# A two-layer graph network: PSUM banks and order of work where one layer hands over to the next

## The chip, the cores and the metric

The kernel runs on one NeuronCore of a Trainium2 chip. The metric is the time of one execution on the device, in microseconds; lower is better. The kernel before takes 3890.02 us (median of three runs, 3889.3 to 3892.25).

## The reference

Eight graphs of 2048 nodes with 256 features share one adjacency matrix. Layer 0 is attention with four heads of 64, in which the softmax is taken separately within each of eight chunks of 256 keys and the chunks' results are added; then come an output projection, a residual and two layer norms. Layer 1 is graph attention with additive scores, a residual and a norm.

```python
# layer 0
q, k, v = x @ Wq.T + bq, x @ Wk.T + bk, x @ Wv.T + bv        # per head
scores = clip(einsum('bhnd,bhjcd->bhnjc', q, kc) / 8, -10, 10)
scores = where(mask == 0, -10, scores)
ctx = einsum('bhnjc,bhjcd->bhnd', softmax(scores, -1), vc)    # softmax per chunk
out = layernorm(ctx @ Wo.T + bo + x) * gamma + beta
x = layernorm(x + out)
# layer 1
Wh = x @ W                                                     # per head
e = leaky_relu(s_src[:, :, None, :] + s_dst[:, None, :, :])    # masked with adj
x = layernorm(x + elu(einsum('bijh,bjhd->bihd', softmax(e, 2), Wh)))
```

## The kernel before

The work goes batch by batch (`b`, eight of them). A batch has 64 slots of layer 0: four blocks of 512 queries, two pairs of heads, eight chunks of keys. In a slot TensorE makes the next slot's scores (L360), VectorE clips and masks them (L371), ScalarE takes the exponential (L383), and TensorE multiplies by the values (`product`, L393), once per head of the pair. `normalize` (L408 to L417) divides by the sums on VectorE and GpSimd. Beside this, each slot carries three tiles of layer 1 of the batch before: VectorE makes `e` (L689), TensorE multiplies (`use`, L709). Layer 1 goes in twelve units; the end of a unit (`close`) has four steps: `dn` on VectorE (L732, L733), `hh` on ScalarE (L737, the last reader of the unit's PSUM bank `pa`), `ee` and `hp` on ScalarE (L741, L743), and `h` on VectorE (L745). `lower.rest(n)` takes n of these steps.

Between the last slot of a batch and the first of the next lies the **change of layers**, written out by hand as a list of steps (`order`). In it the next batch's four blocks are projected (load `l`, turn `t` on VectorE at L274, keys `k` and queries `q` at L304, values `v` at L320, with ScalarE drains at L312 and L327), while the last block of queries of the batch at hand is finished: its context is turned on TensorE and copied by ScalarE (`ctx`, L441 and L444), projected (`po`, L508), added to its input (L519), normed twice (statistics on VectorE at L458 to L467, GpSimd at L468 and L469, apply on ScalarE at L473), turned (`pt`, L283, copied at L286) and multiplied by layer 1's weights (`pw`, L552, drained at L559 and L563). Then `factors` makes layer 1's score factors. The seventh batch is followed by the eighth; after the eighth, layer 1 runs alone, with another list of steps.

Each engine runs its instructions in the order in which the program emits them. [...]`psA` has two tiles of two banks each (scores, the projections, `po`, `pt`, `pw`), `psC` one bank (`product`), `psL` two tiles of one bank (layer 1's `pa`, and at the program's start the masks' `pm`), `psM` one bank. A new tile of a pool waits until the readers of the earlier tile in its place are done.

At the start of the program the first batch's blocks are projected with a step of `Masks` between every two pieces: six or five transposes of the adjacency on TensorE (`pm`, L229), `clip` on VectorE (L231), `edge` on ScalarE (L233), and the next `ab` on VectorE (L219).

Of the kernel before, what the change touches and what calls it, by code (L numbers as in the profile page):

```python
# [8 lines left out]
F32 = mybir.dt.float32  # L9
# [4 lines left out]
AF = mybir.ActivationFunctionType  # L14
# [3 lines left out]
P = 128  # L18
CH = 512
# [3 lines left out]
def adj_resnorm_kernel(  # L23
# [19 lines left out]
    nc = tc.nc  # L43
    B, N, F = x.shape
    H, D = a_src.shape
    NT = N // P
    NCH = N // CH
    KC = F // P
# [7 lines left out]
    QT = CH // P  # L56
# [7 lines left out]
    SLOTS = NCH * QS  # L64
# [17 lines left out]
    psA = ctx.enter_context(tc.tile_pool(name="psA", bufs=2, space=bass.MemoryType.PSUM))  # L82
    psC = ctx.enter_context(tc.tile_pool(name="psC", bufs=1, space=bass.MemoryType.PSUM))
    psL = ctx.enter_context(tc.tile_pool(name="psL", bufs=2, space=bass.MemoryType.PSUM))
# [16 lines left out]
    qT = big.tile([P, KC, N], F32, tag="qT", name="qT")  # L101
    kT = big.tile([P, KC, N], F32, tag="kT", name="kT")
# [30 lines left out]
    wk_sb = weights(wkT, "wk_sb")  # L133
# [155 lines left out]
    def project(b, g):  # L289

        cols = slice(g * CH, (g + 1) * CH)
        st = {}

        def load():
            st["x"] = load_turned(x, b, g, "xp")

        def turn():
            st["xT"] = turned(st["x"], "xT")

        def linear(dst, w, bias):  # L300
            pp = psA.tile([P, KC, CH], F32, tag="psA", name="pp")
            for c in range(KC):
                for kc in range(KC):
                    nc.tensor.matmul(  # L304
                        pp[:, c, :],
                        lhsT=w[:, kc, c * P : (c + 1) * P],
                        rhs=st["xT"][:, kc, :],
                        start=(kc == 0),
                        stop=(kc == KC - 1),
                    )  # L310
            for c in range(KC):
                nc.scalar.activation(  # L312
                    dst[:, c, cols], pp[:, c, :], AF.Identity, bias=bias[:, c : c + 1]
                )

        def values():
            pv = psA.tile([P, QT, F], F32, tag="psA", name="pv")
            for u in range(QT):
                for kc in range(KC):
                    nc.tensor.matmul(  # L320
                        pv[:, u, :],
                        lhsT=st["xT"][:, kc, u * P : (u + 1) * P],
                        rhs=wv_sb[:, kc, :],
                        start=(kc == 0),
                        stop=(kc == KC - 1),
                    )
            nc.scalar.copy(  # L327
                vaug[:, QT * g : QT * (g + 1), :, :D],
                pv.rearrange("p t (h d) -> p t h d", h=H),
            )  # L330

        return [
            load,
            turn,
            lambda: linear(kT, wk_sb, bk_sb),
            values,
            lambda: linear(qT, wq_sb, bq_sb),
        ]


    where = [(s // QS, s % QS // NK, s % NK) for s in range(SLOTS)]
# [60 lines left out]
    def normalize(s):  # L402

        q, hp, c = where[s]
        raw = raws.pop(s)
        del probs[s]
        rd = small.tile([P, 2, QT, 1], F32, tag="rd", name="rd")
        nc.vector.reciprocal(rd, raw[:, :, :, D:D1])  # L408
        if c == 0:
            accs[q, hp] = small.tile([P, QT, 2, D], F32, tag="acc", name="acc")  # L410
        accv = accs[q, hp].rearrange("p t k d -> p k t d")
        part = accv
        if c:
            part = small.tile([P, 2, QT, D], F32, tag="part", name="part", bufs=1)
        nc.gpsimd.tensor_mul(part, raw[:, :, :, :D], rd.to_broadcast([P, 2, QT, D]))  # L415
        if c:
            nc.gpsimd.tensor_add(accv, accv, part)  # L417
# [435 lines left out]
    lower = None  # L853
    for b in range(B):
        waug = blocks.tile([P, NT, H, D1], F32, tag="waug", name="waug")
        sd = small.tile([P, 2 * H, NT], F32, tag="sd", name="sd", bufs=1)
        if b == 0:
            for s in range(3):
                load_slab(s)
        scores(0)  # L860
        for u in range(KT):
            exps(0, u)
        if lower:
            for _ in range(STEP):
                lower.make()
        closing = Closing(b - 2, CLOSING) if b > 1 else None
        if closing:
            closing.do(-1)
        group = None
        for s in range(SLOTS):  # L870
            q, hp, c = where[s]
            i = s % QS
            send()
            if s + 3 < SLOTS:
                load_slab(s + 3)
            if i == 0:
                before = group
                group = Between(b, q - 1, sd, waug) if q else None
            if i == 1 and q:
                load_context(b, q - 1, 1)  # L880
            if i == QS // 2 + 1:
                load_context(b, q, 0)
            if group and i in AHEAD:
                AHEAD[i](group)
            if s == SLOTS - 1 and b + 1 < B:
                turns = [project(b + 1, g) for g in range(NCH)]
                turns[0].pop(0)()
            if s:
                normalize(s - 1)
            if s + 1 < SLOTS:  # L890
                scores(s + 1)

            if i == 3 and q:
                turn_context(q - 1, 1)
            if i == QS // 2 + 3:
                turn_context(q, 0)
            if group:
                for step in BESIDE.get(i, ()):
                    step(group)
            elif closing:  # L900
                closing.do(s, behind=False)
            product(s, 0)
            if s + 1 < SLOTS:
                for u in range(KT):
                    exps(s + 1, u)
            if lower:
                if b + 1 < B or s < SLOTS - LATE:
                    lower.step()
            elif masks.left():
                masks.step()  # L910
            product(s, 1)

            if before and i in AFTER:
                AFTER[i](before)
            if i == 0 and q:
                send_context(b, q - 1, 1)
            if i == QS // 2:
                send_context(b, q, 0)
            if group and i in BEHIND:
                BEHIND[i](group)  # L920
            elif closing and not q:
                closing.do(s, beside=False)
        normalize(SLOTS - 1)
        if lower and b + 1 < B:
            lower.rest(4)

        send()
        before = group
        gd, fs = factors(b, sd, waug)
        group = None  # L930
        every = tuple(range(QT))

        def begin():
            nonlocal group
            group = Between(b, NCH - 1, sd, waug)

        def ctx():
            context(NCH - 1, 1)

        steps = [  # L940
            lambda: group.bias(),
            lambda: group.output(every),
            lambda: group.add(every),
            lambda: (group.shift(), group.a.stats(every)),
            lambda: group.a.apply(group.y),
            lambda: (group.scale(), group.again(), group.b2.stats(every)),
            lambda: group.finish(),
            lambda: group.turn_all(),
            lambda: group.values((0, 1)),
            lambda: group.values((2, 3)),  # L950
        ]
        if b + 1 < B:
            (t0, k0, v0, q0), (l1, t1, k1, v1, q1), (l2, t2, k2, v2, q2), (l3, t3, k3, v3, q3) = turns
            order = [begin, t0, lambda: before.values((2, 3)), steps[0], k0, ctx, l1, v0, steps[1]]
            order += [t1, steps[2], q0, *steps[3:5], k1, l2, steps[5], v1, steps[6], t2, q1, l3]
            order += [steps[7], k2, steps[8], steps[9], v2, fs[0], t3, q2, fs[1], k3]
            order += [lambda: [load_slab(s) for s in range(3)], fs[2], v3, q3]
        else:

            step = lower.step  # L960
            order = [begin, lambda: before.values((2, 3)), steps[0], step, ctx, step, steps[1], step]
            order += [steps[2], step, steps[3], step, steps[4], step, steps[5], step, steps[6], step]
            order += [steps[7], step, steps[8], step, steps[9], step, fs[0], step, fs[1], step, fs[2]]
            order += [step, lambda: lower.rest(4)]
            assert sum(p is step for p in order) == LATE
        for piece in order:
            send()
            piece()
        send()
        lower = Layer1(b, gd, waug)  # L970
# [56 lines left out]
```

## Time and profile before

| what | value |
|---|---|
| time, median of three | 3890.02 us |
| span of the profiled run | 3888.7 us |
| TensorE busy | 3696.5 us |
| VectorE busy | 3204.7 us |
| ScalarE busy | 1946.2 us |
| last change of layers, first `pw` to first product of the next batch | 3178.00 to 3241.86 us |
| keys/queries drain, 128x512 (L312) | 0.683 us each |
| values drain, 128x1024 (L327) | 1.013 us |
| turn of a block on VectorE, 128x1024 (L274) | 1.243 us |

A timeline line gives start and duration in us, engine, line, operation, output and inputs with their shape, and how many instructions are merged; in brackets the time that the engine was idle ahead of it and what ended the wait. TensorE's ends are modelled, so the distance from start to start tells more than a duration does. Names: `pp` is a projection of keys (`wk_sb`) or queries (`wq_sb`), `pv` of values.

### The profile page before, as it was taken

To read this page: it belongs to the slowest core of one execution; us is meant where nothing else is said; L and a number is where in the kernel's file an instruction comes from. 1 tells how busy PE (TensorE), PEld (TensorE's weight loads), DVE (VectorE), ACT (ScalarE), POOL (GpSimd) and SP (SyncE) were. 2 spreads that over 40 slices of the span, in tenths; PEclk is the share of its full clock that TensorE was granted. 3 is DMA by queue.
4 is the path that set the end of the run, shared out by engine and by line. 5 is a ranking of instruction groups with operands and counts; after the bars stand their busy time and mean duration, and the time that the engine had idled before them with its cause. 6 is when DMAs were issued, how large, how long until landed. Compare 5 with 4: busy or idle time off the path is not lost. (4 is left out here: it accounts for less than half of the span.)

```text
span 3888.7 us, 160154 instructions
## 1 busy us (share of the span) xinstructions
PE 3696.5 (95%) x72068; PEld 2752.5 (71%) x72068; DVE 3204.7 (82%) x4810; ACT 1946.2 (50%) x3601; POOL 1384.4 (36%) x1202
## 2 busy tenths in 40 slices
PE   7988999999999999999999999999999999999787
PEld 4655577776777767776777767777677776776676
DVE  4776499985999779996999959998599977998798
ACT  3655445554555445554555545555455555555321
POOL 0444234342433333432433324434243333434310
PEclk9999999999999999999999999999999999999999
DMA  7642333333434343333433334333343334333354
GB/s 151 150 108 59 77 96 98 97 89 94 121 97 102 75 121 101 99 102 70 134 99 100 97 87 129 101 95 88 94 121 102 98 78 118 106 95 88 95 146 123
DMA packets 771328, 398.48 MB, mean 102 GB/s; under 512 B 442576, under 2 KB 735824, under 8 KB 770640
## 3 DMA queue, kind: packets, MB, share of 16 engines
q1 hardware_dynamic: 720640, 354.54, 35.9%
q10 hardware_dynamic: 50000, 33.70, 2.7%
q8 instruction: 563, 9.22, 1.0%
q14 instruction: 125, 1.02, 0.1%
HBM read 331.22 MB, written 56.89 MB: 100 GB/s over the span
## 5 line engine op out<-in xcount | busy, mean ns | idle before, releaser
L371 DVE SCALAR_TENSOR_TENSOR pr<-ps,slab 128x1024 f32<-128x1024 f32 x1024 | 1192.7, 1205 | 237.3 <-PE ps L360 234.0
L393 PEld LDWEIGHTS pc<-vaug,pr 128*64 128x64 f32 x32768 | 1041.6, 138 | 475.3 <-ACT raw L400 243.9
L689 DVE SCALAR_TENSOR_TENSOR e<-srow,gd,et 128x640 f32<-128x640 f32 (+1 forms) x1536 | 1348.0, 934 | 5.4 <-PE pa L709 5.4
L393 PE MATMUL pc<-vaug,pr 128*64 128x65 f32 x32768 | 1161.4, 224 | 68.9 <-ACT raw L400 63.1
L383 ACT ACTIVATE pr<-pr 128x1024 f32<-128x1024 f32 x1024 | 1052.1, 1057 | 249.3 <-DVE pr L371 234.5
L709 PE MATMUL pa<-waug,e 128*64 128x65 f32 x32768 | 1089.8, 224 | 41.0 <-DVE e L689 39.2
L709 PEld LDWEIGHTS pa<-waug,e 128*64 128x64 f32 x32768 | 1025.2, 139 | 70.3 <-DVE e L689 39.8
L360 PE MATMUL ps<-qT,kT 64*128 64x512 f32 x4096 | 1022.4, 617 | 9.1 <-DVE pr L371 7.0
L415 POOL TENSOR_TENSOR part<-raw,rd 128x512 f32<-128x512 f32 x448 | 467.9, 1044 | 1472.7 <-DVE rd L408 1460.1
L400 ACT COPY raw<-pc 128x260 f32<-128x260 f32 x1024 | 383.5, 375 | 1139.0 <-PE pc L393 1092.4
L417 POOL TENSOR_TENSOR acc<-acc,part 128x512 f32<-128x512 f32 x448 | 574.0, 1281 | 35.2
L360 PEld LDWEIGHTS ps<-qT,kT 64*128 64x128 f32 x4096 | 351.5, 186 | 332.1 <-issue 208.7
L408 DVE RECIPROCAL rd<-raw 128x8 f32<-128x8 f32 x512 | 101.5, 198 | 139.4 <-ACT raw L400 133.2
L415 POOL TENSOR_TENSOR acc<-raw,rd 128x512 f32<-128x512 f32 x64 | 66.8, 1043 | 366.1 <-DVE rd L408 365.3
L304 PE MATMUL pp<-xT,wk_sb 128*128 128x512 f32 x256 | 123.9, 628 | 47.0 <-DVE xT L274 32.3
L737 ACT ACTIVATE hh<-pa,dn 128x64 f32<-128x64 f32 x512 | 114.0, 319 | 101.3 <-DVE dn L733 101.3
L552 PE MATMUL pw<-w_sb,x1T 128*128 128x264 f32 x512 | 137.0, 403 | 2.6 <-DVE x1T L274 2.5
L468 POOL TENSOR_TENSOR rs_c<-rs_c,nhalf 128x4 f32<-128x4 f32 x32 | 55.6, 1738 | 227.5 <-DVE off_c L467 227.5
L508 PE MATMUL po<-wo_sb,qT 128*128 128x256 f32 x512 | 124.8, 389 | 0.0
L304 PEld LDWEIGHTS pp<-xT,wk_sb 128*128 128x128 f32 x256 | 48.3, 198 | 106.5 <-issue 49.6
L320 PE MATMUL pv<-wv_sb,xT 128*128 128x256 f32 x512 | 115.9, 379 | 0.0
L304 PE MATMUL pp<-xT,wq_sb 128*128 128x512 f32 x256 | 115.3, 593 | 0.0
(90 smaller groups left out, 1888.2 us busy)
## 6 DMA issues: line engine op xcount, KB each, us to landing
et<-edgeD SPq DMA_DIRECT2D x256, 320.0 KB, 3.2
slab<-clipD SPq DMA_DIRECT2D x512, 128.0 KB, 3.5
et<-edgeD SPq DMA_DIRECT2D x128, 384.0 KB, 3.5
srow<-rowD SPq DMA_DIRECT2D x64, 320.0 KB, 4.4
xp<-in_x_dram SPq DMA_DIRECT2D x256, 64.0 KB, 2.3
xg<-in_x_dram SPq DMA_DIRECT2D x32, 512.0 KB, 4.7
x1D<-y ACTq DMA_DIRECT2D x32, 512.0 KB, 3.1
x1g<-x1D SPq DMA_DIRECT2D x32, 512.0 KB, 5.9
```

Of the source, the lines that this page charges most:

```text
L304: nc.tensor.matmul(pp[:, c, :], lhsT=w[:, kc, c * P : (c + 1) * P], rhs=st["xT"][:, kc, :], start=(kc == 0), stop=(kc == KC - 1),)
L360: nc.tensor.matmul(ps[:, k, :], lhsT=kT[rows, hp, t * P : (t + 1) * P], rhs=qT[rows, hp, cols], start=True, stop=True,)
L371: nc.vector.scalar_tensor_tensor(pr, pss[u], -CLIP, slab[:, u, :].unsqueeze(1).to_broadcast([P, 2, CH]), op0=ALU.max, op1=ALU.min,)
L383: nc.scalar.activation(pr, pr, AF.Exp, scale=0.125)
L393: nc.tensor.matmul(pc[z * D : (z + 1) * D, i, :], lhsT=probs[s][u][:, k, i * P + z * D : i * P + (z + 1) * D], rhs=vaug[:, KT * c + u, 2 * ...
L400: nc.scalar.copy(raws[s][:, k], pc)
L415: nc.gpsimd.tensor_mul(part, raw[:, :, :, :D], rd.to_broadcast([P, 2, QT, D]))
L417: nc.gpsimd.tensor_add(accv, accv, part)
L508: nc.tensor.matmul(po[:, k, :], lhsT=qT[:, c, t * P : (t + 1) * P], rhs=wo_sb[:, c, :], start=(c == 0), stop=(c == KC - 1),)
L552: nc.tensor.matmul(pw[:, k, : F + 2 * H], lhsT=self.x1T[:, c, u * P : (u + 1) * P], rhs=w1_sb[:, c, :], start=(c == 0), stop=(c == KC - 1),)
L689: nc.vector.scalar_tensor_tensor(e[:, :w], self.rows[n][:, :w], self.gd[:, h, j : j + 1], self.edge[k // JG][:, j % JG, :w], op0=ALU.max, ...
L709: nc.tensor.matmul(self.pa[z * D : (z + 1) * D, i * D1 : (i + 1) * D1], lhsT=e[:, i * P + z * D : i * P + (z + 1) * D], rhs=self.waug[:, j ...
```

## The change

Four things are done together, all at the change of layers. Values and queries leave `psA` and go through layer 1's two one-bank tiles (`psL`), half a block at a time, each half drained as soon as its matmuls are done; keys stay in `psA`, also drained half by half. The first block of the next batch is loaded at slot 61 rather than 63 and turned in slot 63, ahead of the change. The end of layer 1's last unit, which was taken in one go ahead of the change, is spread over it. And `normalize` of the last slot moves behind the first keys. The aim is that TensorE should not wait for the first turn nor for the drains of the two-bank tiles. The same `project` also serves the first batch at the program's start, where `psL` carries the masks.

```diff
-        def linear(dst, w, bias):
+        def linear(dst, w, bias, c, pp):
+            for kc in range(KC):
+                nc.tensor.matmul(pp, lhsT=w[:, kc, c * P : (c + 1) * P], rhs=st["xT"][:, kc, :], ...)
+            nc.scalar.activation(dst[:, c, cols], pp, AF.Identity, bias=bias[:, c : c + 1])
+
+        def keys():
             pp = psA.tile([P, KC, CH], F32, tag="psA", name="pp")
             for c in range(KC):
-                for kc in range(KC):
-                    nc.tensor.matmul(pp[:, c, :], ...)
-            for c in range(KC):
-                nc.scalar.activation(dst[:, c, cols], pp[:, c, :], ...)
+                linear(kT, wk_sb, bk_sb, c, pp[:, c, :])
+
+        def queries():
+            for c in range(KC):
+                linear(qT, wq_sb, bq_sb, c, psL.tile([P, CH], F32, tag="psL", name="pq"))
 
         def values():
-            pv = psA.tile([P, QT, F], F32, tag="psA", name="pv")
-            for u in range(QT):
-                ...
-            nc.scalar.copy(vaug[:, QT * g : QT * (g + 1), :, :D], ...)
+            for u0 in range(0, QT, 2):
+                pv = psL.tile([P, 2, F], F32, tag="psL", name="pv")
+                for u in range(2):
+                    ...
+                t = QT * g + u0
+                nc.scalar.copy(vaug[:, t : t + 2, :, :D], ...)
...
-            if s == SLOTS - 1 and b + 1 < B:
+            if s == SLOTS - 3 and b + 1 < B:
                 turns = [project(b + 1, g) for g in range(NCH)]
                 turns[0].pop(0)()
             if s:
                 normalize(s - 1)
+            if s == SLOTS - 1 and b + 1 < B:
+                turns[0].pop(0)()
             if s + 1 < SLOTS:
                 scores(s + 1)
...
-        normalize(SLOTS - 1)
-        if lower and b + 1 < B:
-            lower.rest(4)
...
-            order = [begin, t0, lambda: before.values((2, 3)), steps[0], k0, ctx, l1, v0, steps[1]]
+            rest = [lambda: lower.rest(1)] if lower else []
+            norm = lambda: normalize(SLOTS - 1)
+            order = [begin, *rest, k0, norm, lambda: before.values((2, 3)), *rest, l1, v0, *rest, ctx]
+            order += [steps[0], steps[1], *rest]
             order += [t1, steps[2], q0, *steps[3:5], k1, l2, steps[5], v1, steps[6], t2, q1, l3]
             order += [steps[7], k2, steps[8], steps[9], v2, fs[0], t3, q2, fs[1], k3]
```

In the list, `steps[0]` adds the output bias to the input, `steps[1]` is the output product `po`, `steps[2]` the add, `steps[3:5]` the first norm, `steps[5]` scale, second residual and its statistics, `steps[6]` the second norm's apply and the store, `steps[7]` the turn `pt`, `steps[8]` and `steps[9]` the two halves of `pw`, and `fs` the factors.

More of the change, by code (lines that the diff above doesn't have):

```diff
@@ L298, in turn @@
             st["xT"] = turned(st["x"], "xT")
-        def linear(dst, w, bias):
+        def linear(dst, w, bias, c, pp):
+            for kc in range(KC):
+                nc.tensor.matmul(
+                    pp,
+                    lhsT=w[:, kc, c * P : (c + 1) * P],
+                    rhs=st["xT"][:, kc, :],
+                    start=(kc == 0),
+                    stop=(kc == KC - 1),
+                )
+            nc.scalar.activation(dst[:, c, cols], pp, AF.Identity, bias=bias[:, c : c + 1])
@@ L301, in linear @@
+        def keys():
             pp = psA.tile([P, KC, CH], F32, tag="psA", name="pp")
             for c in range(KC):
-                for kc in range(KC):
[L304 to L310, printed above, removed]
-            for c in range(KC):
-                nc.scalar.activation(
-                    dst[:, c, cols], pp[:, c, :], AF.Identity, bias=bias[:, c : c + 1]
-                )
@@ L316, in values @@
-        def values():
-            pv = psA.tile([P, QT, F], F32, tag="psA", name="pv")
-            for u in range(QT):
[L319 to L338, printed above, removed]
+                linear(kT, wk_sb, bk_sb, c, pp[:, c, :])
+        def queries():
+            for c in range(KC):
+                linear(qT, wq_sb, bq_sb, c, psL.tile([P, CH], F32, tag="psL", name="pq"))
+        def values():
+            for u0 in range(0, QT, 2):
+                pv = psL.tile([P, 2, F], F32, tag="psL", name="pv")
+                for u in range(2):
+                    for kc in range(KC):
+                        nc.tensor.matmul(
+                            pv[:, u, :],
+                            lhsT=st["xT"][:, kc, (u0 + u) * P : (u0 + u + 1) * P],
+                            rhs=wv_sb[:, kc, :],
+                            start=(kc == 0),
+                            stop=(kc == KC - 1),
+                        )
+                t = QT * g + u0
+                nc.scalar.copy(
+                    vaug[:, t : t + 2, :, :D], pv.rearrange("p t (h d) -> p t h d", h=H)
+                )
@@ L341, in adj_resnorm_kernel @@
+        return [load, turn, keys, values, queries]
     where = [(s // QS, s % QS // NK, s % NK) for s in range(SLOTS)]
@@ L952, in adj_resnorm_kernel @@
         if b + 1 < B:
-            (t0, k0, v0, q0), (l1, t1, k1, v1, q1), (l2, t2, k2, v2, q2), (l3, t3, k3, v3, q3) = turns
-            order = [begin, t0, lambda: before.values((2, 3)), steps[0], k0, ctx, l1, v0, steps[1]]
+            (k0, v0, q0), (l1, t1, k1, v1, q1), (l2, t2, k2, v2, q2), (l3, t3, k3, v3, q3) = turns
+            rest = [lambda: lower.rest(1)] if lower else []
+            norm = lambda: normalize(SLOTS - 1)
+            order = [begin, *rest, k0, norm, lambda: before.values((2, 3)), *rest, l1, v0, *rest, ctx]
+            order += [steps[0], steps[1], *rest]
             order += [t1, steps[2], q0, *steps[3:5], k1, l2, steps[5], v1, steps[6], t2, q1, l3]
@@ L960, in adj_resnorm_kernel @@
             step = lower.step
+            normalize(SLOTS - 1)
             order = [begin, lambda: before.values((2, 3)), steps[0], step, ctx, step, steps[1], step]
```

## The prediction

> **What bounds the kernel now.** I read the page's first part, then the timeline of TensorE around the seven changes of layers, then VectorE's and ScalarE's there, and last the start of the program.
>
> ```profile
> PE 3696.5 (95%) x72068; PEld 2752.5 (71%) x72068; DVE 3204.7 (82%) x4810; ACT 1946.2 (50%) x3601; POOL 1384.4 (36%) x1202
> ```
>
> TensorE is busy 95% of the span; only its idle time can be won. One change of layers (the last) on TensorE, number in brackets the idle time ahead and its releaser:
>
> ```profile
> 3178.00 2.94 PE L552 MATMUL pw<-w_sb,x1T 128*128 128x264 f32 x12
> 3183.26 3.70 PE L304 MATMUL pp<-xT,wk_sb 128*128 128x512 f32 x8 [2.32 <-DVE xT L274]
> ...
> 3190.69 3.62 PE L508 MATMUL po<-wo_sb,qT 128*128 128x256 f32 x16
> 3194.14 3.60 PE L304 MATMUL pp<-xT,wq_sb 128*128 128x512 f32 x8
> 3199.10 3.70 PE L304 MATMUL pp<-xT,wk_sb 128*128 128x512 f32 x8 [1.35 <-ACT qT L312]
> ...
> 3211.79 3.70 PE L304 MATMUL pp<-xT,wk_sb 128*128 128x512 f32 x8 [0.94 <-ACT qT L312]
> ...
> 3238.34 2.16 PE L360 MATMUL ps<-qT,kT 64*128 64x512 f32 x8 [0.30 <-ACT qT L312]
> 3240.80 1.13 PE L360 MATMUL ps<-qT,kT 64*128 64x512 f32 x4 [0.30 <-DVE pr L371]
> ```
>
> Five gaps, 2.32 + 1.35 + 0.94 + 0.30 + 0.30 = 5.2 us. Six of the seven changes show the same five within 0.02 us; the first has no layer 1 beside it and other gaps. Everything the change could win is 6 x 5.2 + 2.6 = 34 us, 0.9%.
>
> The first gap on VectorE: xT stands behind `h`, which waited 2.50 us for ScalarE (layer 1's end, taken in one go).
>
> ```profile
> 3174.99 0.19 DVE L408 RECIPROCAL rd<-raw 128x8 f32<-128x8 f32 x1
> 3178.60 0.20 DVE L408 RECIPROCAL rd<-raw 128x8 f32<-128x8 f32 x1 [3.41 <-ACT raw L400]
> ...
> 3181.56 0.49 DVE L745 SCALAR_TENSOR_TENSOR h<-ee,hp 128x320 f32<-128x320 f32 x1 [2.50 <-ACT hp L743]
> 3181.97 1.24 DVE L274 STREAM_TRANSPOSE xT<-xp 128x1024 f32<-128x1024 f32 x1
> ```
>
> The third gap on ScalarE: the drain of q1, for whose bank k2 waits, stands behind the norm's apply.
>
> ```profile
> 3207.95 2.08 ACT L473 ACTIVATE y<-y,off_b,rs_b 128x256 f32<-128x256 f32 x4 [0.65 <-POOL off_b L469]
> 3210.47 1.26 ACT L312 ACTIVATE qT<-pp,bq_sb 128x512 f32<-128x512 f32 x2 [0.44 <-ACT y L473]
> ```
>
> The first change of layers, where gap two is missing:
>
> ```profile
> 427.33 3.60 PE L304 MATMUL pp<-xT,wq_sb 128*128 128x512 f32 x8
> ...
> 441.80 0.33 PE L283 MATMUL pt<-identf,y 128*128 128x128 f32 x1 [0.55 <-ACT y L473]
> ...
> 444.98 5.19 PE L304 MATMUL pp<-xT,wk_sb 128*128 128x512 f32 x8 [0.94 <-ACT qT L312]
> ```
>
> From the end of the output product (start of q0, call it P) to k2 is 444.98 - 427.33 = 17.65 us here and 3211.79 - 3194.14 = 17.65 us there. With gap two TensorE reaches `pt` when y is there; without it, it waits for y. So **gap two is hidden**: what sets this stretch is the chain add, stats, apply, scale, stats, apply, turn, which starts at P.
>
> **What the skill says.** The Trainium skill, "PSUM — Partial Sum Buffer", Engine vs sequencer instructions: ScalarE and VectorE queues are strict first in, first out, and matmuls run in program order. The trace agrees: the drain at 3210.47 was ready at 3209.7 (q1's matmuls end) and went behind apply and the store's issue. The same page, PSUM bank collisions raise a hardware error: two engines may not touch one bank at a time, so guard by bank. That is why two one-bank tiles can be filled and drained in turn. "Perfetto Trace Analysis", Tensor Engine Instruction: ends on TensorE are a model. So I count start to start: 8 matmuls of 592 ns pass in 3.45 us (3190.69 to 3194.14 for the 16 of `po` likewise), a half in 1.73.
>
> **The change, part by part** (last change of layers; the five others are alike).
>
> Turning block 0 in slot 63: 1.24 us of VectorE after `rd` at 3174.99, in the 3.41 us in which it idled; its eight loads were issued by 3171.6 and land 2.1 us after (median of that view), about 3174. Taken out of an idle stretch, it costs nothing. The load's move to slot 61 changes nothing: SyncE issued it straight behind x1t's, which wait for x1D. xT is there at 3176.5, so k0 starts when slot 63's four `pw` matmuls are through: 3178.0 + 4 x 0.231 = 3178.9. Gap one is gone.
>
> New order on TensorE: k0 to 3182.45; before.values, 8 x 0.231, to 3184.3; first half of v0 to 3186.03. The second half needs layer 1's bank, whose last reader is `hh`. ScalarE in order: kT halves (0.68 each) to 3183.3; waug and sd (0.57 + 0.12) 3184.5 to 3185.2; hh (1.15) to 3186.3. So the second half starts 3186.36: **0.33 us of new wait**. It ends 3188.1; ctx's four transposes to 3188.5; `po`'s first pair to 3188.96. Its next pair needs ctx's copy, and ahead of that on ScalarE stand v0's second drain (0.59, 3188.3 to 3188.9), ee and hp (0.83, to 3189.7), then the copy (0.59, to 3190.2). Before, v0 lay between ctx and output and hid it; now nothing does: **1.3 us of new wait**. Behind it on TensorE stand the rest of `po`, q0 and k1, and VectorE's add waits for `po`, so it moves all that follows. The remaining 14 of 16 matmuls, 3.02 us, give P = 3193.27 against 3194.14: **gain 0.87**.
>
> From P the chain is unchanged: add, two norms and `h` or t1 ahead of add are done long before. Queries no longer hold psA, so gap two goes, but TensorE then waits for y at `pt`: worth nothing. `pt` ends at P + 16.6, k2 takes the bank of k1, drained by P + 9, and starts there rather than at P + 17.65: **gain 1.0**. The pw after it needs x1T's copy, about P + 18.5, and k2 runs to P + 20: hidden. Later pieces ran without gaps and shift.
>
> At the end q3 no longer stands in a psA bank ahead of scores(0): the two 0.30 gaps shrink to about 0.35 (the wait for `pr` stays): **gain 0.25**.
>
> Per change 0.87 + 1.0 + 0.25 = 2.12, six times 12.7. In the first change no gap one and no tail: k0 starts as before, but ctx's copy is bare: v0's second drain and the copy, 0.55 us after `po`'s first pair; -0.55 + 1.0 + 0.25 = +0.7.
>
> Splitting v's drain: two of 0.59 (row L559, 128x512) for one of 1.01; 0.17 more on a ScalarE that is 50% busy; hidden.
>
> The program's start pays, because there psL carries the masks' `pm`:
>
> ```profile
> 36.06 0.50 PE L229 MATMUL pm<-identb,ab 128*128 128x128 bf16 x6
> 36.40 3.67 PE L320 MATMUL pv<-wv_sb,xT 128*128 128x256 f32 x16
> 36.60 0.96 DVE L231 TENSOR_SCALAR clip<-pm 128x768 int8<-128x768 bf16 x1 [2.96 <-PE pm L229]
> 37.64 0.80 ACT L233 CAST edge<-pm 128x768 uint8<-128x768 bf16 x1
> ```
>
> v's second half would start at 36.40 + 1.73 = 38.13 and gets the `pm` bank at 38.44: 0.3. After the next `pm` (0.4) q's first half waits for v's second drain, 0.59 + 0.2 after its matmuls: 0.45. In the four blocks 0.45 + 0.8 + 0.55 + 0.55 = **2.4 us lost**; behind each of these waits on TensorE stands the next `pm`, for which clip, `ab` and the next block's turn wait on VectorE, and the slots after (about 4.7 us each, TensorE with gaps below 0.6) have nothing to absorb it. Bounds: 0 to 4.
>
> The last batch's order is the same; normalize only stands in another place of the source.
>
> Sum: 12.7 + 0.7 - 2.4 = 11.0. 3890.0 - 11.0 = **3879.0 us**.
>
> **Rivals.**
> - *More of the gaps goes* (chance 0.12). If the tile after hh and ctx's copy came sooner (the steps of layer 1's end beside other work, as placed), P gains up to 2.32: 3.57 x 6 + 1.3 - 2 = 21, 3869. For: ScalarE is half idle. Against: its order is fixed and puts v0's drain, ee and hp ahead of the copy. Even all 34 us would be 3856.
> - *The new wait takes the place of the old* (0.22). If hh and ctx's copy cost what gap one did (2.3 rather than 1.6, say each hop 0.3 later), only 1.0 + 0.25 is left: 1.25 x 6 + 0.5 - 2.4 = 5.6, 3884; with 4 lost at the start, 3886. Within 0.2%.
> - *Slower: two single banks are too few* (0.11). If one 0.68 us drain per piece is bare, 8 pieces x 0.68 = 5.4 us a change and as much at the start: 8 x 5.4 - 13 = +30, 3920; half of it 3898; likewise if k2's tile lands in `pt`'s bank and waits for x1T's copy (P + 18.5 for 17.65, 0.85 lost instead of 1.0 won). For: each tile now waits two back, half as much matmul time (1.73) as before. Against: 1.73 exceeds 0.68 + 0.2, and ScalarE is held up only at apply, after which no psL tile is asked for until v2.
> - *The forecast* (0.55): 3879.
>
> Range: 3867 to 3889 takes in the forecast with its bounds, most of the first rival and the second. Below 3882.2 (0.2%) lie the forecast, the first rival and little of the second: faster 0.62, same 0.26, slower 0.12.
>
> **What would show it.** Right: no DVE xT wait ahead of the first k; a wait of `po` for ctx's qT copy of 1 to 1.5 us; waits of `pt` for y of about 1 us and k2 straight after; P to k2 about 16.6; scores(0) at some 75.7 us rather than 73.3. Wrong: `po` without that wait, P to k2 still 17.65 (another bank chosen), q or v halves waiting for qT or vaug drains inside the change of layers, or a start as long as before.

## The result, and the profile after

The kernel after takes 3927.81 us (median of four runs, 3925.04 to 3930.74), the kernel before 3891.14 us on the same chip (median of four): a ratio of 1.0094, 95% interval 1.0077 to 1.0112. It is 37 us slower, where 11 us faster was forecast.

The first part of its page:

```profile
PE 3719.1 (95%) x72068; PEld 2758.4 (70%) x72068; DVE 3202.9 (82%) x4810; ACT 1958.3 (50%) x3633; POOL 1390.3 (35%) x1202
```

TensorE runs the same 72068 instructions, yet is busy 22.6 us longer (3696.5 before). The span grew by 38.1 us, so the other 15.5 us are more idle time. Two things went wrong, not one: TensorE waits more, and some of the same matmuls take longer.

TensorE's waits, first of the kernel before, then of the kernel after (engine, what waits, releaser: us in total, times, longest us):

```profile
PE pp L304 <- DVE xT L274: 32.3, 10, 16.3
PE pp L304 <- ACT qT L312: 14.7, 13, 1.4
...
PE ps L360 <- ACT qT L312: 2.1, 7, 0.3
```

```profile
PE pp L302 <- ACT kT L309: 42.4, 32, 3.3
...
PE pp L302 <- DVE xT L274: 18.6, 4, 16.6
...
PE po L507 <- ACT qT L443: 6.3, 7, 1.0
...
PE pq L302 <- ACT vaug L333: 1.5, 4, 0.4
```

What the change was to remove is gone: 13.7 us of waiting for `xT`, and the waits for the two-bank tiles of queries (14.7 + 2.1 us). The forecast wait of `po` for the context's copy has come, 1.0 us in six changes and 0.3 us in the first. But the largest of the new entries was not in the forecast: keys wait for keys' own drain, 32 times, 42.4 us. There are 32 blocks of keys in the program, so every one waits once.

The last change of layers on TensorE, the same stretch as in the prediction:

```profile
3211.45 1.16 PE L551 MATMUL pw<-w_sb,x1T 128*128 128x264 f32 x4
3212.44 1.88 PE L302 MATMUL pp<-xT,wk_sb 128*128 128x512 f32 x4
3215.10 1.99 PE L302 MATMUL pp<-xT,wk_sb 128*128 128x512 f32 x4 [0.78 <-ACT kT L309]
...
3218.70 3.94 PE L325 MATMUL pv<-wv_sb,xT 128*128 128x256 f32 x16
...
3224.52 3.29 PE L507 MATMUL po<-wo_sb,qT 128*128 128x256 f32 x14 [1.01 <-ACT qT L443]
3227.64 3.60 PE L302 MATMUL pq<-xT,wq_sb 128*128 128x512 f32 x8
3231.08 1.88 PE L302 MATMUL pp<-xT,wk_sb 128*128 128x512 f32 x4
3236.23 3.68 PE L302 MATMUL pp<-xT,wk_sb 128*128 128x512 f32 x4 [3.28 <-ACT kT L309]
3239.75 3.62 PE L325 MATMUL pv<-wv_sb,xT 128*128 128x256 f32 x16
3243.20 3.60 PE L302 MATMUL pq<-xT,wq_sb 128*128 128x512 f32 x8
3246.64 1.04 PE L283 MATMUL pt<-identf,y 128*128 128x128 f32 x8
3247.51 1.88 PE L302 MATMUL pp<-xT,wk_sb 128*128 128x512 f32 x4
```

A block of keys is now two lines of four matmuls. The second half waits for the drain `kT` of the first, 0.78 us in the first block (3212.44 to 3215.10 is 2.66 us, where a half passes in 1.73) and 3.28 us in the second block (5.15 us from half to half). And the half behind the long wait is slow: four matmuls show 3.68 us instead of 1.99.

ScalarE shows why the second block's wait is longer (in brackets the idle time ahead and what ended it):

```profile
3233.53 2.07 ACT L472 ACTIVATE y<-y,off_a,rs_a 128x256 f32<-128x256 f32 x4 [1.57 <-POOL off_a L468]
3235.51 0.67 ACT L309 ACTIVATE kT<-pp,bk_sb 128x512 f32<-128x512 f32 x1
```

The first half of k1 was multiplied by about 3232.9. Its drain stands behind the first norm's apply in ScalarE's queue; the apply waits for its statistics until 3233.53 and takes 2.07 us. So the drain starts at 3235.51, and TensorE goes on 0.05 us after its end. The strict order of ScalarE that the prediction took from the Trainium skill ("PSUM — Partial Sum Buffer", Engine vs sequencer instructions) holds here too; it was applied to the drain of q1 and not to that of k1.

The granted TensorE clock around that wait, in three windows that follow each other (from and to, length; busy time of TensorE and its instructions; clock as a share of full speed; DMA share; GB/s):

```profile
3232.90:3236.31 3.41, 0.13 (x2) 1.00 0.00 0
3236.31:3239.72 3.41, 3.41 (x4) 0.50 0.13 20
3239.72:3243.13 3.41, 3.41 (x17) 1.00 0.78 123
```

After 3.28 us of idleness the clock is halved for 3.41 us, just where the second half of the keys runs (3236.23 to 3239.75).

The first gap is gone on VectorE too: `xT` follows `rd` at once, and `h`, which held it up before, now comes 15 us after it and delays nothing on TensorE.

```profile
3208.43 0.19 DVE L407 RECIPROCAL rd<-raw 128x8 f32<-128x8 f32 x1
3208.54 1.19 DVE L274 STREAM_TRANSPOSE xT<-xp 128x1024 f32<-128x1024 f32 x1
...
3224.02 0.49 DVE L744 SCALAR_TENSOR_TENSOR h<-ee,hp 128x320 f32<-128x320 f32 x1 [10.68 <-ACT hp L742]
```

At the program's start the first scores come at 84.66 us instead of 73.29: 11.4 of the 38.1 us. The rest, 26.7 us, is in the seven changes of layers, 3.8 us each on average (4.3 in the last).

### The profile page after: what moved, and what is told of

Same layout as the page of the kernel before. It is cut to its first block, busy times and chain, and to the rows that moved or that the text cites. A ratio compares the mean times of both kernels' runs of the same rounds, so it can differ in the third digit from the quotient of the medians.

```text
span 3926.8 us, 160146 instructions
## 1 busy us (share of the span) xinstructions
PE 3719.1 (95%) x72068; PEld 2758.4 (70%) x72068; DVE 3202.9 (82%) x4810; ACT 1958.3 (50%) x3633; POOL 1390.3 (35%) x1202
## 5 line engine op out<-in xcount | busy, mean ns | idle before, releaser
L302 PE MATMUL pp<-xT,wk_sb 128*128 128x512 f32 x256 | 140.9, 678 | 61.0 <-ACT kT L309 42.4
L325 PEld LDWEIGHTS pv<-wv_sb,xT 128*128 128x128 f32 x512 | 98.7, 196 | 25.9 <-issue 9.2
```

The source lines that it names most:

```text
L302: nc.tensor.matmul(pp, lhsT=w[:, kc, c * P : (c + 1) * P], rhs=st["xT"][:, kc, :], start=(kc == 0), stop=(kc == KC - 1),)
L325: nc.tensor.matmul(pv[:, u, :], lhsT=st["xT"][:, kc, (u0 + u) * P : (u0 + u + 1) * P], rhs=wv_sb[:, kc, :], start=(kc == 0), stop=(kc == K ...
```

## The experiments

The theory (T): the loss is the half-by-half drain of the keys. The two halves share one two-bank tile of `psA`, and the second half's matmuls wait for ScalarE's read of the first half, although it is of another bank. Where this wait is long, the clock falls too. Without it the change would win what the prediction said. The rivals: the two one-bank tiles of `psL` are too few, as the prediction's slower case had it; or the new order and the spread end of layer 1 are what costs; and, for the slow half, that it is not the clock falling after idleness but something that goes with the place.

Five marks serve for comparison in the last change: start (first `pw`), P (start of q0), k2, and `ps`, the next batch's first scores; and the first scores of the program.

| kernel | first scores | start to P | P to k2 | k2 to `ps` | start to `ps` |
|---|---|---|---|---|---|
| before | 73.29 | 16.14 | 17.65 | 25.12 | 58.91 |
| after | 84.66 | 16.19 | 19.87 | 27.12 | 63.18 |
| keys drained whole | 79.63 | 15.15 | 16.54 | 25.02 | 56.71 |
| turn alone | 75.17 | 13.55 | 17.66 | 25.13 | 56.34 |
| context ahead of values | 73.77 | 13.55 | 16.53 | 25.03 | 55.11 |
| wait for `y` filled | 74.00 | 13.55 | 13.94 | 26.00 | 53.49 |

**Keys drained whole.** The kernel after; both halves of the keys are multiplied first and then drained, as before the change. Nothing else differs.

```diff
             for c in range(KC):
-                linear(kT, wk_sb, bk_sb, c, pp[:, c, :])
+                products(wk_sb, c, pp[:, c, :])
+            for c in range(KC):
+                drain(kT, bk_sb, c, pp[:, c, :])
```

> The changed kernel, with one thing undone: the two halves of the keys are again drained after all eight of their matmuls (as in the kernel before), everything else as changed. Theory T (the second half of the keys waits for the drain of the first, because both halves lie in one PSUM tile; at the second block that drain stands behind the norm's apply, TensorE idles 3.28 us and then runs at half its clock): the waits of pp for kT go, 4 x 0.78 at the start and 3 x 0.78 + 3.28 in each of seven changes, 42 us, and with them the slow halves, some 1.8 to 2.9 us each, so 3928 - 42 - 10 to 17: about 3870 to 3877, near the forecast of 3879. Rival R1 (layer 1's two banks, shared by values, queries, masks and pa, are what costs): the kT waits are only where the wait shows, time stays above 3905. Rival R2 (waits go, but the lower clock has another cause and stays): about 3886.

Measured: 3877.66 us, ratio to before 0.9964 (0.9951 to 0.9977): 50 us less than after. The same stretch of TensorE:

```profile
3181.73 3.60 PE L302 MATMUL pq<-xT,wq_sb 128*128 128x512 f32 x8
3185.16 3.60 PE L302 MATMUL pp<-xT,wk_sb 128*128 128x512 f32 x8
3188.59 3.62 PE L333 MATMUL pv<-wv_sb,xT 128*128 128x256 f32 x16
3192.05 3.60 PE L302 MATMUL pq<-xT,wq_sb 128*128 128x512 f32 x8
3196.19 0.33 PE L283 MATMUL pt<-identf,y 128*128 128x128 f32 x1 [0.55 <-ACT y L480]
```

k1 is one line of eight matmuls again, and v1 starts 3.43 us after it, not 8.67. The waits for `kT` are gone from the table, all 42.4 us. What comes back is `pt`'s wait for `y`, which the prediction had foreseen and which k1's delay had covered in the kernel after. As causes of the net loss the bank pool and the new order fall with this run: `psL`, the order and the spread end are all still there. (What they cost within it, at the program's start and ahead of `po`, is told further down.)

**Keys in two tiles.** The kernel after; each half of the keys is still drained at once, but has a tile of `psA` to itself.

```diff
-            pp = psA.tile([P, KC, CH], F32, tag="psA", name="pp")
             for c in range(KC):
-                linear(kT, wk_sb, bk_sb, c, pp[:, c, :])
+                linear(kT, wk_sb, bk_sb, c, psA.tile([P, CH], F32, tag="psA", name="pp"))
```

> The changed kernel, keys still drained half by half, but each half in a psA tile of its own. Theory T: what binds the two halves is the common tile, not the early drain; so no pp waits for kT between the halves and the time is that of the kernel with whole keys, plus up to 0.3 us per change where the second half of the third block takes pt's bank: 3870 to 3880. Rival R3 (a drain put between the halves holds TensorE whatever the tile, for instance because both write kT): as the changed kernel, about 3928.

Measured: 3881.18 us, ratio 0.9974 (0.9962 to 0.9986). Three blocks of the last change, k0, k1 and k2, and the first drain of k0:

```profile
3171.18 3.60 PE L302 MATMUL pp<-xT,wk_sb 128*128 128x512 f32 x8
3173.10 0.69 ACT L309 ACTIVATE kT<-pp,bk_sb 128x512 f32<-128x512 f32 x1 [1.27 <-PE pp L302]
...
3188.77 3.60 PE L302 MATMUL pp<-xT,wk_sb 128*128 128x512 f32 x8
...
3201.86 3.99 PE L302 MATMUL pp<-xT,wk_sb 128*128 128x512 f32 x8
```

Draining early is not at fault; draining out of a tile that is still being filled is. With two tiles k1 passes without a gap although its first drain still stands behind the apply. In k0 the first drain runs (from 3173.10, for 0.69 us) while the second half is multiplied (from 3172.89), and the block takes the same 3.60 us: here TensorE filled one bank while ScalarE read another. In the kernel after the two halves also lay in different banks, but in one tile, and waited; so the wait came with the tile, not with the bank. In k2 the second half needs the place of `pt`, and its 0.39 us (3.99 for 3.60) is the wait for that copy. The early drain gained nothing either: with the keys drained whole the time was 3877.66 us.

**The long wait filled.** The kernel after; in the seven changes three matmuls are put between the two halves of k1, into a bank of `psM`. Nobody reads their result.

```diff
             for c in range(KC):
+                if c and b and g == 1:
+                    pf = psM.tile([P, CH], F32, tag="psM", name="pf")
+                    for _ in range(3):
+                        nc.tensor.matmul(pf, lhsT=wk_sb[:, 0, :P], rhs=st["xT"][:, 0, :], ...)
                 linear(kT, wk_sb, bk_sb, c, pp[:, c, :])
```

> The changed kernel with work added: three matmuls of 128x512 (2.6 us, their result is read by nobody) between the two halves of the second block's keys in the seven changes of layers, where TensorE idles 3.28 us. Theory T with the clock (the idle time lowers the clock for what follows): the clock stays at 1.00, the second half takes 1.73 us instead of 3.52 and values keep 3.45: 1.8 to 2.9 us saved in each of seven changes, 3928 - 13 to 20 = 3908 to 3915, though work was added. Rival R5 (the slow half has another cause than the idle time): 3928, or a little more.

Measured: 3914.81 us, ratio 1.0058 (1.0043 to 1.0073), 13.0 us less than after with more work to do. TensorE, and below it the window of k1's second half:

```profile
3220.20 2.74 PE L317 MATMUL pf<-xT,wk_sb 128*128 128x512 f32 x6
3223.65 1.98 PE L302 MATMUL pp<-xT,wk_sb 128*128 128x512 f32 x4 [0.71 <-ACT kT L309]
3225.47 3.62 PE L331 MATMUL pv<-wv_sb,xT 128*128 128x256 f32 x16
```

```profile
3223.60:3225.40 1.80, 1.75 (x4) 1.00 0.00 0
```

The wait for `kT` still ends at the same event, but TensorE is idle for only 0.71 us of it, the clock stays at 1.00, and the half takes 1.98 us in all seven changes. In the kernel after, from the start of this half to the start of q1 takes 5.28 us in the one change where it is not slow, and 6.87 to 8.29 us in the other six: together 12.5 us more, close to the 13.0 us won here. So the place is not the cause: it is the same, only the idleness went.

**Turn alone.** The kernel before, with one part of the change: block 0 is loaded at slot 61 and turned in slot 63.

```diff
-            if s == SLOTS - 1 and b + 1 < B:
+            if s == SLOTS - 3 and b + 1 < B:
                 turns = [project(b + 1, g) for g in range(NCH)]
                 turns[0].pop(0)()
             if s:
                 normalize(s - 1)
+            if s == SLOTS - 1 and b + 1 < B:
+                turns[0].pop(0)()
...
-            order = [begin, t0, lambda: before.values((2, 3)), steps[0], k0, ctx, l1, v0, steps[1]]
+            order = [begin, lambda: before.values((2, 3)), steps[0], k0, ctx, l1, v0, steps[1]]
```

> The kernel before, with one part of the change alone: block 0 is loaded at slot 61 and turned in slot 63; no PSUM tile moves, layer 1's end stays in one go, normalize stays where it was. By the trace of before the first gap of 2.32 us goes in six changes and all that follows starts that much earlier: 3890 - 13.9 = 3876. Rival R4 (something else is ready no earlier, the add or ctx's copy, and the gap only moves): 3886 to 3890.

Measured: 3872.03 us, ratio 0.9949 (0.9933 to 0.9966).

```profile
3162.69 2.94 PE L552 MATMUL pw<-w_sb,x1T 128*128 128x264 f32 x12
3165.46 3.60 PE L304 MATMUL pp<-xT,wk_sb 128*128 128x512 f32 x8
...
3181.20 3.70 PE L304 MATMUL pp<-xT,wk_sb 128*128 128x512 f32 x8 [1.36 <-ACT qT L312]
```

The first gap (2.32 us) is gone, the second (1.36 us) stays, and P comes 2.59 us earlier. The six later changes give 15.5 us of the 19.6 measured. Another 1.7 us is clock: in the kernel before, one of the six blocks behind the 2.32 us gap is slow:

```profile
876.67 5.40 PE L304 MATMUL pp<-xT,wk_sb 128*128 128x512 f32 x8 [2.32 <-DVE xT L274]
...
1339.29 3.70 PE L304 MATMUL pp<-xT,wk_sb 128*128 128x512 f32 x8 [2.32 <-DVE xT L274]
```

Eight matmuls, the same wait, 5.40 us against 3.70. In the two profiled runs the first change gives 1.9 us more and the program's start takes 1.9 us back; the remaining 2 us or so were not traced.

**Banks alone.** The kernel before, with values and queries through `psL` in halves and nothing else: no early turn, layer 1's end in one go, normalize where it was, the old order, keys drained whole.

```diff
-            if s == SLOTS - 3 and b + 1 < B:
+            if s == SLOTS - 1 and b + 1 < B:
                 turns = [project(b + 1, g) for g in range(NCH)]
                 turns[0].pop(0)()
...
+            order = [begin, t0, lambda: before.values((2, 3)), steps[0], k0, ctx, l1, v0, steps[1]]
```

(The diff is against the run with keys drained whole; only its main lines are shown.)

> The kernel before, with another part of the change alone: values and queries through layer 1's two banks, half by half; keys whole in psA, block 0 turned where it was, layer 1's end in one go. By the prediction's steps the start loses 2.4 us, the third gap (0.94) goes and the two of 0.30 shrink, 1.25 per change, while the first (2.32) stays and TensorE waits at pt for y: 3891 + 2.4 - 7 x 1.25 = 3885, within 0.2%. Rival R1 (the two banks are too few): above 3900.

Measured: 3888.67 us against 3889.05, ratio 0.9999 (0.999 to 1.0008). The first scores come at 78.61 us, 5.3 later than before, and the seven changes win about as much (6.7 us in the profiled run). The 0.94 us gap and the second gap have gone, but the gap that remains now costs more:

```profile
3179.78 5.40 PE L302 MATMUL pp<-xT,wk_sb 128*128 128x512 f32 x8 [2.33 <-DVE xT L274]
```

k0 behind the same 2.33 us wait is slow here in four of the six changes that have this gap (one of six before). So two one-bank tiles are not too few: they are neutral on the whole, with a loss at the start.

**Start in psA.** The run with keys drained whole; in addition the first batch's projections, at the program's start, use `psA` as before the change.

```diff
+        if b == 0:
+            return [load, turn, lambda: linear_whole(kT, wk_sb, bk_sb),
+                    values_whole, lambda: linear_whole(qT, wq_sb, bq_sb)]
         return [load, turn, keys, values, queries]
```

> The kernel with whole keys (3877.7), and the first batch's projections at the program's start once more in psA, as before the change. If the masks' pm and the halves get in each other's way at the start, as predicted, the 2.3 to 2.7 us there come back: 3875. Rival R6 (slots after it had absorbed it, or the start is set by loads): 3878.

Measured: 3870.39 us, ratio 0.9954 (0.9939 to 0.9968). The intervals of this run and of the one it builds on overlap; the mark is clearer: the first scores come at 74.43 us, not 79.63. That is 5.2 us, where 2.3 to 2.7 were expected.

**Context ahead of values.** In addition `ctx` stands ahead of v0 in the list, so that v0's matmuls lie between the context's turn and the output product.

```diff
-            order = [begin, *rest, k0, norm, lambda: before.values((2, 3)), *rest, l1, v0, *rest, ctx]
+            order = [begin, *rest, k0, norm, lambda: before.values((2, 3)), *rest, l1, ctx, v0, *rest]
```

> As the one before, and the turn of the context moved ahead of block 0's values, so that they hide its copy as they did before the change. By the forecast's arithmetic the wait of po for qT (1.01 us measured) and the 0.33 us in front of the values' second half go: 1.3 us in six changes, 0.3 in the first: 3875 - 8 = 3867. Rival R7 (the chain through y is bound elsewhere, and the gain turns into a longer wait at pt): 3874.

Measured: 3861.42 us, ratio 0.9929 (0.9914 to 0.9944), 9.0 us less than without it.

```profile
3158.29 0.60 PE L488 MATMUL pt<-identf,acc 128*128 128x128 f32 x4
3158.73 3.62 PE L333 MATMUL pv<-wv_sb,xT 128*128 128x256 f32 x16
3162.18 3.62 PE L555 MATMUL po<-wo_sb,qT 128*128 128x256 f32 x16
3165.64 3.60 PE L302 MATMUL pq<-xT,wq_sb 128*128 128x512 f32 x8
```

`po` is one line of sixteen matmuls without a wait. The wait of v0's second half went as well: 3.62 us, where 3.94 stood in the kernel after, because `ctx` gives `hh` the time it lacked. Start to P falls from 15.15 to 13.55 us.

**Wait for `y` filled.** In addition k2 moves ahead of `pt`, which waits for `y`, and the first half of v2 goes between `pt` and `pw`.

```diff
-        def values():
-            for u0 in range(0, QT, 2):
+        def values(halves=(0, 2)):
+            for u0 in halves:
...
-            order += [steps[7], k2, steps[8], steps[9], v2, fs[0], t3, q2, fs[1], k3]
+            order += [k2, steps[7], lambda: v2((0,)), steps[8], steps[9], lambda: v2((2,))]
+            order += [fs[0], t3, q2, fs[1], k3]
```

> As the one before, and the wait of pt for y filled: the third block's keys ahead of pt, and the first half of its values between pt and layer 1's product, which hides the copy of x1T; nothing is left out. From the start of q0 the third keys then begin after 13.8 us rather than 16.5, and about 1.8 us per change are won if nothing else binds: 3867 - 7 x 1.8 = 3854. Rival R8 (the factors' chain, through rowD to layer 1's first srow, comes too late and takes it back): 3860 to 3867.

Measured: 3849.62 us, ratio 0.9899 (0.9885 to 0.9914).

```profile
3165.99 3.60 PE L302 MATMUL pq<-xT,wq_sb 128*128 128x512 f32 x8
3169.61 3.70 PE L302 MATMUL pp<-xT,wk_sb 128*128 128x512 f32 x8
3173.15 1.04 PE L283 MATMUL pt<-identf,y 128*128 128x128 f32 x8
3174.02 1.89 PE L333 MATMUL pv<-wv_sb,xT 128*128 128x256 f32 x8
3175.75 3.72 PE L599 MATMUL pw<-w_sb,x1T 128*128 128x264 f32 x16
```

None of these lines carries a wait. P to k2 is 2.59 us shorter because k2 now comes first; 0.97 us of it comes back from k2 to `ps`, where `pt` now lies, and 1.62 us per change are won (about 1.8 were expected). This version beats the kernel before by 1.0% and the kernel after by some 76 us (0.9899 against 1.0094); it keeps all four parts of the change, without the keys' half drain and without `psL` at the start.

## Why the prediction was wrong

**The step that failed** is the first of "New order on TensorE": "k0 to 3182.45", and likewise every other block of keys. It took eight matmuls in 3.45 us, as before, and never costed that keys are now drained half by half inside one two-bank tile. In its ScalarE order the halves of `kT` stand as work for ScalarE and are costed there; that TensorE would wait for the first of them was not asked. The reason it gave for one-bank tiles, that they can be filled and drained in turn, is the very one that a two-bank tile drained in part lacks. Measured: 0.78 us at 25 of the 32 blocks and 3.28 us at the seven that are k1 of a change of layers, 42.4 us in all, where 0 was assumed.

**The sum, corrected** for the last change, kernel after against keys drained whole (the two differ in this alone). Start to P, 1.04 us more: all of it is k0, which takes 4.48 us for 3.44 (0.93 from its first half to its second, 2.66 for 1.73, and 0.11 after it). P to k2, 3.33 us more: k1 takes 8.67 us for 3.43, of which 3.42 is the wait (5.15 for 1.73) and 1.69 the slow clock (6.97 for 5.28 from its second half to q1), and 1.91 comes back, because `y` is ready by then and `pt` no longer waits (q1 to k2 takes 4.31 us for 6.22). k2 to `ps`, 2.10 us more: k2 takes 4.48 us for 3.43 and k3 4.58 for 3.54. Together 6.5 us; at the start 5.0 us more, 3.7 of it four halves. 7 x 6.5 + 5.0 = 50.5 us; the profiled spans differ by 3926.8 - 3875.2 = 51.6.

**The clock** was no term of the prediction at all. An idle gap was priced at its length, here 3.28 us, and cost 1.6 to 3.0 us more in six of seven changes. Its "only its idle time can be won" fails for the same reason: busy time was lost too. The Trainium skill, "TensorE: Matmul & The Clock Gate", What's actually happening, states that the clock is halved after an idle window of about 3.4 us, and that these windows run freely. The traces agree on the windows: the falls of the clock in the kernel after at 447.62, 1372.63, 2304.47 and 3236.31 us are 271, 273 and 273 times 3.413 us apart, and the falls in the changes of layers last one or two windows. They do not agree that the window must be idle throughout. Windows of the kernel after around a 3.28 us gap without a slow half, then of the banks alone around a 2.32 us gap with a slow block:

```profile
905.01:908.43 3.42, 1.42 (x4) 1.00 0.00 0
908.43:911.84 3.41, 2.14 (x6) 1.00 0.00 0
```

```profile
3176.71:3180.12 3.41, 1.08 (x5) 1.00 0.00 0
3180.12:3183.53 3.41, 3.41 (x5) 0.50 0.50 79
```

What separates the cases is how the gap lies to the windows. There are nineteen gaps of 2.3 or 3.3 us at the changes of layers in the kernels before, after and with the banks alone. In eleven of them the clock fell, each time at the end of a window that held 1.98 us or more of the gap; in the other eight the gap was shared between two windows, and neither held more than 2.00 us of it. Nor is one long gap needed: the prediction's own lines show a slow block of keys (444.98, 5.19 us where others take 3.70) behind a gap of 0.94 us, at the end of a window with several short gaps in which TensorE was busy for 1.81 of 3.41 us. The exact limit is not shown.

**What held.** With keys drained whole the kernel is what the prediction thought the kernel after to be, and it takes 3877.66 us; 3879.0 was forecast. The six later changes fit the forecast's own terms; that the total fits as well as it does is partly luck, as two misses cancel in the profiled runs: the start lost 6.3 us for 2.4, and the first change won 3.9 us for 0.7.

- Start to P: 15.27 forecast (3193.27 - 3178.00, with a slip of 0.1 us in it: 3178.9 + 3.45 is 3182.35, not 3182.45), 15.15 measured. The wait for `hh`: 0.33 forecast, 0.32 measured (3.94 for 3.62). The wait for the context's copy: 1.3 forecast, 1.01 measured.
- P to k2: 16.6 forecast, 16.54 measured, with `pt`'s wait for `y` in it. "Gap two is hidden" was right: the chain of the norms sets this stretch, and it took moving k2 ahead of `pt` to shorten it (13.94).
- k2 to `ps`: 0.25 forecast, 0.10 measured. Per change 2.12 forecast, 2.20 measured.
- The start: 2.4 us forecast as waits in `psL`. The waits agree (1.5 us of q for `vaug`, some 0.7 of values' second halves), but the loss is 6.3 us: two more key blocks run at the halved clock than before (33.02 and 64.84 us, 5.4 and 5.3 us for 3.7), 3.3 us of the loss. This size was wrong. That the clock falls there is not the work of `psL` alone: with the turn alone, whose start is the same code as before, the block at 61.03 us is slow (5.40 us) behind the same 0.70 us wait after which the kernel before passes at 60.85 us in 3.70. How much of the 3.3 us is such chance was not separated.

**The rivals.** The slower case had the right sign, and its 3920 lies near the result, but for another cause: "two single banks are too few" is refuted as the cause by the banks alone (0.9999). The prediction also credited little to the early turn: it let 0.87 us of the 2.32 us gap reach P (0.99 did, with the keys drained whole), because the new order put a 1.0 us and a 0.3 us wait in its place. The turn alone brings 0.5%; all four parts with the keys drained whole bring no more (0.4%, and the intervals overlap).

## What to carry to other kernels

Draining a piece early is free only if the piece has a tile of its own: here the matmuls into the second half of a tile were made to wait for the reader of the first, bank or no bank. (That it gains anything, no run here shows.) For each wait that a new drain can cause, ask what stands ahead of that drain in its engine's queue; here it was a norm that waited for its own statistics. And do not price an idle gap of TensorE of 2 to 3 us at its length: depending on where it lies, the matmuls behind it ran at half clock, and in one run even matmuls nobody needs paid.

## What the runs showed of the hardware that was not expected

- A TensorE gap of 3.28 us halved the clock (0.50 granted, for 3.41 or 6.83 us) in six of seven cases and cost 12.5 us in all; filling 2.6 us of it with 42 matmul instructions whose result nobody reads kept the clock at 1.00 and saved 13.0 us.
- A gap of 2.32 us did the same in one of six cases in one kernel and in four of six in another. The falls lie on a grid of 3.41 us, and in these nineteen cases the clock fell when about 2 us or more of the gap lay within one window of it.
- ScalarE can drain one bank of PSUM while TensorE fills another, 3.60 us for a block of keys with its first drain under way (k0) or still due (k1): the 0.78 us wait of the kernel after came from the shared tile.
